# Four graph-attention layers on one core: folding by TensorE, and an order written out for ScalarE and TensorE in the list stage

## The chip, the core and the metric

The kernel runs on one core of a Trainium2 chip. The core has five engines that run side by side and meet at semaphores: TensorE (PE; its weight loads are shown as PEld), VectorE (DVE), ScalarE (ACT), GpSimd (POOL) and SyncE (SP), which here only issues DMAs. Each engine works through its own instructions in order. ScalarE's queue issues DMAs too. The metric is the time of one execution on the device in microseconds; smaller is better. The profile shows one execution, and line numbers such as L698 are those of the kernel before.

## The reference

There are N = 3327 nodes with 512 features and a symmetric adjacency matrix with about 17 entries a row, with ones on the diagonal. Four attention layers follow each other. Each computes

```
h = relu(layernorm(x))
v = h @ W                                  # per head
e[i, j] = leaky_relu(s_src[i] + s_dst[j])  # s_src = v . a_src, s_dst = v . a_dst, per head
x = x + softmax over the neighbours j of i (e) @ v     # layers 1 and 2 pass it through elu
```

with 8, 4, 1 and 8 heads. Since `s_src` is linear in `h`, it can be had as `h @ (W a_src)`: a product of the weights with the attention vectors, done once, gives eight more weight columns for each of the two vectors. The kernel calls this folding.

## The kernel before

Rows are padded to 3328 = 26 tiles of 128. The kernel has a list stage and then, if no row has too many neighbours, four layers that gather neighbours' rows by lists. Only the list stage and the folding of layer 0 are touched by the change.

**The list stage** runs once over the 26 tiles. For tile t SyncE loads 128 rows of the adjacency matrix (`a`, 1664 KB, three buffers; L697). GpSimd multiplies it by descending numbers (`key`, three buffers; L698), so that a row's largest keys name its neighbours. VectorE adds a boost to the diagonal block (L702) and takes the eight largest of each of 16 segments (L707). The 40 largest of those candidates (`top`, L662 and L664) are found in the next tile's loop: the pieces of `rest` stand between the sixteen maxima of the tile after. ScalarE counts the row's ones (L704, with an accumulator) and copies the list (L632, L633). VectorE marks the row's length in one of 41 bins (L640), TensorE counts rows by length with four small products (L642 to L646; the profile shows each product of fp32 as two records), ScalarE copies the running count `sofar` (L649), and VectorE picks each row's place (L654) one tile later still. A buffer of `a` is free again when L698 and L704 have read it.

**Beside the lists**, the same loop computes layer 0's projection. ScalarE's queue loads the tile's x (L726) into one of five row buffers `vx`, ScalarE takes mean and variance (L488 to L495), TensorE transposes (L454), ScalarE cuts at zero (`hT`, L461), TensorE multiplies by the weights (L472), GpSimd raises the variance to the power -1/2 (`root`, L434), ScalarE scales the product by it (L683, L685) and SyncE stores the row to the table `tabx` (L687), from which layer 0 gathers later. In iteration t this is written for tile t-1, behind the maxima of tile t. The weights come in iteration 1 and are folded right there by VectorE: eight times a multiply (L408) and a sum (L410) before tile 2.

**What sets the order.** Inside `with tc.manual_schedule(engines=...)` the engines named keep the order of the source. In the list stage these are GpSimd and VectorE. The order of the others (TensorE, ScalarE, SyncE) is chosen at compile time by a planner that estimates when each instruction is ready. In iteration t GpSimd's order is product t, then the root of t-1. After the loop VectorE finishes the last tile's list and the running count becomes the base of each bin (L738), then ranks, then the lists by rank (L781 to L791). The first gather of layer 0 (L838) needs those.

Of the kernel before, what the change touches and what calls it, by code (L numbers as in the profile page):

```python
# [25 lines left out]
BANK = 512  # L26
# [354 lines left out]
class Weights:  # L381

    def __init__(self, nc, pool, work, l, ws, avs):
# [5 lines left out]
        self.av = pool.tile([P, 2, F], F32, name="av", bufs=1)  # L391
        for s in range(2):
            nc.sync.dma_start(self.w[:, :, s, :HF],
                              ws[l][:, s * HF:(s + 1) * HF].rearrange("(k p) n -> p k n", p=P))
            nc.sync.dma_start(self.av[:, s, :], bass.AP(tensor=avs[l].tensor, offset=avs[l].offset + s * F,
                                                        ap=[[0, P], [1, F]]))
        if self.H < 8:
            nc.vector.memset(self.w[:, :, :, HF + self.H:], 0.0)
        self.left = [(s, k) for s in range(2) for k in range(KC)]

    def fold(self):

# [27 lines left out]
def rooted(nc, ve, small, half=None):  # L430

    if half is not None:
        rstd = small.tile([P, 1], F32, name="root")
        nc.gpsimd.tensor_tensor(rstd, ve, half, OP.pow)  # L434
# [12 lines left out]


def turned(nc, xn, ident, ps_t):

    KC = xn.shape[1] // P
    pt = ps_t.tile([P, KC, P], F32, name="pt")
    for k in range(KC):
        nc.tensor.transpose(pt[:, k, :], xn[:, k * P:(k + 1) * P], ident)  # L454
    return pt


def cut(nc, pt, work):
# [66 lines left out]


@with_exitstack
def tile_gat_stack(ctx: ExitStack, tc: tile.TileContext, x, adj, adjT, ws, avs, out):

# [9 lines left out]
    nc = tc.nc  # L539
    NP, F = x.shape  # L540
    N = adjT.shape[0]
    NT = NP // P
# [21 lines left out]
    with ExitStack() as c1:  # L564
# [19 lines left out]
        nc.scalar.activation(boost, ident, AF.Copy, scale=BOOST)  # L584
# [53 lines left out]
        def sorted_in(t):  # L638
            nonlocal sofar, count
            nc.vector.tensor_scalar(o[:, t, :], bins, held[:, t:t + 1], None, OP.is_equal)  # L640
            pn = ps_n.tile([P, BANK], F32, name="pn", bufs=1)
            nc.tensor.matmul(pn[:, :BINS], upper, o[:, t, :], start=True, stop=False)  # L642
            nc.tensor.matmul(pn[:, :BINS], ident, sofar, start=False, stop=True)
            count = ps_n.tile([P, BANK], F32, name="count", bufs=1)[:, :BINS]
            nc.tensor.matmul(count, ones, o[:, t, :], start=True, stop=False)
            nc.tensor.matmul(count, ident, sofar, start=False, stop=True)  # L646
            if t < NT - 1:
                sofar = once.tile([P, BINS], F32, name="sofar", bufs=2)
                nc.scalar.activation(sofar, count, AF.Copy)  # L649
            return pn  # L650

        def placed(t, pn):
# [27 lines left out]
        def features(t, vx, xn, ve):  # L680
            pv = projected(nc, W, cut(nc, turned(nc, xn, ident, ps_t), work), ps_v)
            rstd = rooted(nc, ve, small, half)
            nc.scalar.activation(vx[:, :ROW].rearrange("p (s n) -> p s n", s=2), pv[:, :, :ROW // 2], AF.Copy,  # L683
                                 scale=rstd)
            nc.scalar.activation(vx[:, ROW + F:].rearrange("p (s n) -> p s n", s=2), pv[:, :, ROW // 2 - 8:ROW // 2],  # L685
                                 AF.Copy, scale=rstd)
            nc.sync.dma_start(tabx[t * P:(t + 1) * P, :], vx)  # L687

        rows = [once.tile([P, 2 * ROW], F32, name=f"vx{i}") for i in range(5)]
        count, pieces, last, normed = None, [], None, None  # L690
        with tc.manual_schedule(engines={mybir.EngineType.Pool, mybir.EngineType.DVE}):
            for t in range(NT):
                a = apool.tile([P, NP], I32, name="a")
                key = kpool.tile([P, NP], I32, name="key")
                quarter = NP // 4 if t == 0 else NP
                for c in range(0, NP, quarter):
                    nc.sync.dma_start(a[:, c:c + quarter], adj[t * P:(t + 1) * P, c:c + quarter])  # L697
                    nc.gpsimd.tensor_tensor(key[:, c:c + quarter], a[:, c:c + quarter], keys[:, c:c + quarter], OP.mult)  # L698
                if t == 1:
                    W = Weights(nc, wpool, work, 0, ws, avs)  # L700
                dg = key[:, t * P:(t + 1) * P]
                nc.vector.tensor_add(dg, dg, boost)  # L702
                waste = once.tile([P, NP], mybir.dt.bfloat16, name="waste")
                nc.scalar.activation(waste, a, AF.Relu, accum_out=total[:, t:t + 1])  # L704
                cand = small.tile([P, SEGS * 8], F32, name="cand")
                for g in range(SEGS):
                    nc.vector.max(cand[:, g * 8:(g + 1) * 8], key[:, g * SEG:(g + 1) * SEG])  # L707
                    if g == SEGS // 2 and last is not None:
                        last()
                        last = None  # L710
                    elif g > 0 and pieces:
                        pieces.pop(0)()
                if t == 0:
                    constants()
                if t == 1:
                    while W.left:
                        W.fold()
                if t == 2:
                    own = late_constants()
                if t > 0:  # L720
                    last = then
                pieces, then = rest(t, cand)

                vx = rows[t % 5]
                xt = vx[:, ROW:ROW + F]
                nc.scalar.dma_start(xt, x[t * P:(t + 1) * P, :])  # L726
                if normed is not None:
                    features(*normed)
                normed = (t, vx, *centred_by_scalar(nc, xt, small, work))
            features(*normed)  # L730
# [754 lines left out]
```

## Time and profile before

| what | value |
|---|---|
| time, median of 3 runs | 2424.75 us (2415.73 to 2427.66) |
| time of the profiled execution | 2419.54 us |
| its span | 2417.8 us |
| PE busy | 2068.3 us (86%) |
| DVE busy | 1885.1 us (78%) |
| POOL busy | 1739.5 us (72%) |
| ACT busy | 936.3 us (39%) |
| first product L698 of the list stage starts | 5.20 us |
| last product L698 starts, takes | 233.80 us, 7.28 us |
| base of the bins (L738) | 253.44 us |
| first gather (L838) | 271.24 us |

In the profile a line gives an engine, the line of the kernel, the operation with what it writes and reads, and a count; "idle before" is the time in which the engine stood still just before, with the instruction that let it go. "issue" is time in which the engine waited for nothing that the profile shows. Busy shares are means over stages with different limits, so the list stage is read by itself.

### The profile page before, as it was taken

How to read it: one execution, taken by the hardware profiler on the slowest of the kernel's cores; microseconds unless marked ns; L12 is line 12 of the kernel's file. 1: busy time of each engine (PE TensorE's matmuls, PEld its weight loads, DVE VectorE, ACT ScalarE, POOL GpSimd, SP SyncE). 2: the span in 40 equal slices, each digit the busy share in tenths (PEclk: the TensorE clock that was granted, in tenths of full speed). 3: DMA queues.
4: the chain of work that ended last, by engine and by line, in shares of the span. 5: the costliest groups of instructions: out<-in, count | busy, mean ns of one | idle time of the engine just before them, and what ended most of it. 6: DMA issues, size and time to landing. Idle time of an engine off the chain costs nothing.

```text
span 2417.8 us, 27489 instructions
## 1 busy us (share of the span) xinstructions
PE 2068.3 (86%) x7298; PEld 1197.0 (50%) x7298; DVE 1885.1 (78%) x4857; ACT 936.3 (39%) x2528; POOL 1739.5 (72%) x1717
## 2 busy tenths in 40 slices
PE   2778779888988885898999987899898699999997
PEld 1656334444444432454455544456565465556653
DVE  7988788877777763888888884888878578888886
ACT  5777113434331111433333332544443444344430
POOL 7899267777777776766677772778778467777775
PEclk9988899999999997999999998999999899999999
DMA  5887569999998788887888884889887578888885
GB/s 227 316 299 248 153 192 299 276 299 282 286 283 237 234 231 241 242 245 235 234 261 255 256 237 141 270 262 283 268 248 240 161 226 256 250 243 246 252 241 176
DMA packets 260732, 594.23 MB, mean 246 GB/s; under 512 B 103699, under 2 KB 121107, under 8 KB 256214
## 3 DMA queue, kind: packets, MB, share of 16 engines
q0 software_dynamic: 124368, 432.13, 59.5%
q1 hardware_dynamic: 132454, 153.45, 19.6%
q10 hardware_dynamic: 3744, 6.82, 0.8%
q8 instruction: 59, 0.97, 0.2%
q14 instruction: 107, 0.88, 0.1%
HBM read 542.60 MB, written 49.65 MB: 245 GB/s over the span
## 4 chain that ended last, share of the span: by engine, by line
DVE 31%; DMA 17%; PE 16%; issue 13%; POOL 12%; ACT 9%; DVEq 0%; SPq 0%; ACTq 0%; POOLq 0%
DVE m L931 13%; POOL g L838 8%; DMA g<-tab,idxb 6%; PE bank L936 5%; DMA g<-tabx,twiceb 4%; PE pv L472 4%; PE whole L1173 3%; POOL key L698 3%; DVE bank L924 3%; ACT r L1280 2%; DMA g<-tab,idxa 2%; DVE room L1296 2%; DVE z L902 2%; ACT pw L903 2%; DVE z L900 1%
## 5 line engine op out<-in xcount | busy, mean ns | idle before, releaser
L936 PE MATMUL bank<-m,ident 128*128 128x512 f32 x2414 | 1128.0, 613 | 144.8 <-DVE m L931 144.3
L838 POOL DMA_INDIRECT g<-tab,idxb x712 | 683.1, 959 | 236.0 <-issue 162.0
L931 DVE TENSOR_TENSOR m<-g,pw 128x512 f32<-128x512 f32 x1207 | 752.2, 682 | 100.2 <-ACT pw L903 99.6
L936 PEld LDWEIGHTS bank<-m,ident 128*128 128x128 f32 x2414 | 448.7, 194 | 689.2 <-issue 314.6
L472 PE MATMUL pv<-w,hT 128*128 128x264 f32 x1664 | 431.5, 413 | 67.8 <-ACT hT L461 44.5
L903 ACT ACTIVATE pw<-z 128x32 f32<-128x32 f32 (+4 forms) x356 | 68.2, 191 | 988.9 <-DVE z L902 988.9
L472 PEld LDWEIGHTS pv<-w,hT 128*128 128x128 f32 x1664 | 331.7, 203 | 166.8 <-ACT hT L461 50.8
L838 POOL DMA_INDIRECT g<-tab,idxa x297 | 286.3, 964 | 165.0 <-issue 110.6
L838 POOL DMA_INDIRECT g<-tabx,twiceb x342 | 324.0, 947 | 106.0 <-issue 79.5
L1173 PE MATMUL whole<-ve,em 128*128 128x512 f32 x468 | 217.8, 612 | 16.3 <-DVE em L1152 11.2
L698 POOL TENSOR_TENSOR key<-a,keys 128x3328 int32<-128x3328 int32 (+1 forms) x29 | 189.3, 6530 | 16.3 <-DVE cand L707 11.8
L924 DVE SCALAR_TENSOR_TENSOR bank<-g,L,bank 128x512 f32<-128x512 f32 x243 | 183.3, 754 | 6.8
L900 DVE TENSOR_TENSOR z<-g,pw 128x32 f32<-128x32 f32 (+4 forms) x356 | 62.6, 176 | 152.1 <-DMA g<-tabx,twiceb 64.7
L1314 PEld LDWEIGHTS whole<-L,room 128*128 128x128 f32 x1248 | 147.5, 190 | 24.9 <-issue 19.1
L838 POOL DMA_INDIRECT g<-tabx,twicea x99 | 94.9, 959 | 78.5 <-issue 38.1
L1314 PE MATMUL whole<-L,room 128*128 128x130 f32 x1248 | 147.8, 274 | 0.0
L707 DVE MAX8 cand<-key 128x8 f32<-128x208 int32 x416 | 144.0, 364 | 0.1
L1173 PEld LDWEIGHTS whole<-ve,em 128*128 128x128 f32 x468 | 88.1, 196 | 109.2 <-issue 87.2
L1280 ACT ACTIVATE r<-low,L 128x384 f32<-128x384 f32 x208 | 121.2, 583 | 5.1
L454 PE MATMUL pt<-ident,xn 128*128 128x128 f32 x416 | 65.4, 281 | 35.4 <-ACT hT L461 13.6
L454 PEld LDWEIGHTS pt<-ident,xn 128*128 128x128 f32 x416 | 52.5, 145 | 68.6 <-issue 28.3
L931 DVE TENSOR_TENSOR bank<-g,pw 128x512 f32<-128x512 f32 x74 | 51.5, 696 | 37.4 <-ACT pw L903 36.6
(180 smaller groups left out, 2192.6 us busy)
## 6 DMA issues: line engine op xcount, KB each, us to landing
a<-in_adj SPq DMA_DIRECT2D x25, 1664.0 KB
tab<-v SPq DMA_DIRECT2D x78, 264.0 KB
ve<-tab SPq DMA_DIRECT2D x78, 264.0 KB
g<-tab SPq DMA_DIRECT2D x65, 264.0 KB
tabx<-vx SPq DMA_DIRECT2D x26, 528.0 KB
g<-tab,idxb POOLq DMA_INDIRECT x712, 4.0
low<-tab SPq DMA_DIRECT2D x52, 132.0 KB
spare<-tab SPq DMA_DIRECT2D x52, 132.0 KB
```

The costliest lines, as they stand in the source:

```text
L454: nc.tensor.transpose(pt[:, k, :], xn[:, k * P:(k + 1) * P], ident)
L472: nc.tensor.matmul(pv[:, s, :HF + 8], hT[:, k, :], W.w[:, k, s, :], start=(k == 0), stop=(k == KC - 1))
L698: nc.gpsimd.tensor_tensor(key[:, c:c + quarter], a[:, c:c + quarter], keys[:, c:c + quarter], OP.mult)
L707: nc.vector.max(cand[:, g * 8:(g + 1) * 8], key[:, g * SEG:(g + 1) * SEG])
L838: nc.gpsimd.indirect_dma_start(out=out_, out_offset=None, in_=table, in_offset=bass.IndirectOffsetOnAxis(ap=which, axis=0))
L903: nc.scalar.activation(self.wt[:, k0:k0 + n, :H], z, AF.Exp)
L924: nc.vector.scalar_tensor_tensor(acc, v, w, acc, OP.mult, OP.add)
L931: nc.vector.tensor_tensor(out_.rearrange("p (s h d) -> p s h d", s=2, d=D), v.rearrange("p s (h d) -> p s h d", d=D), wt[:, k0 + q, :H].re ...
L936: nc.tensor.matmul(self.po, ident, m[:, q, :], start=False, stop=(k0 + q == K - 1), skip_group_check=True)
L1173: nc.tensor.matmul(tl.po.rearrange("p (s m) -> p s m", s=2), e[:, q * P:(q + 1) * P], v.rearrange("p (s m) -> p s m", s=2)[:, :, :F // 2], ...
L1280: nc.scalar.activation(self.r[:, h, :], self.a[:, g, :], AF.Relu, bias=-1.0, scale=self.b[:, j, g:g + 1])
L1314: nc.tensor.matmul(dst, e[:, h, q * P:(q + 1) * P], mov, start=False, stop=(j == NT - 1), skip_group_check=True)
```

## The change

There are three parts.

1. *Folding.* `Weights` gets an argument `turned`. With it no attention vectors are spread over all partitions by DMA; instead the weights are loaded a second time in the other orientation (`wT`, into the buffer `low`, which is not used yet), with a small block-diagonal matrix of the attention vectors (`spread`, made from the inputs like the other rearrangements). `multiply` forms the folded columns by 16 products on TensorE and four copies on ScalarE. It is used for layer 0; the other layers fold as before.
2. *Order.* The whole list stage keeps the source's order on ScalarE and TensorE too, which were the planner's. The source is rearranged for that: the boost first, x of tile t+1 issued in iteration t, projection of t-1 ahead of tile t's maxima, tile t's row total and centring behind it. SyncE stays with the planner.
3. *Later store.* The root, the scaling and the store of a row move from tile t-1 to tile t-2, and so does the copy of the running count, out of `sorted_in` into `passed`. Roots follow product t on GpSimd.

```diff
@@ class Weights
+        if turned is not None:
+            room, wT, spread = turned
+            self.wT = room[:, :KC * F].rearrange("p (c f) -> p c f", c=KC)
+            self.spread = room[:, KC * F:KC * F + KC * 4].rearrange("p (c a) -> p c a", c=KC)
+            nc.sync.dma_start(self.spread, spread.rearrange("p (c a) -> p c a", c=KC))
+            nc.sync.dma_start(self.wT, wT.rearrange("(c p) f -> p c f", p=P))
...
+    def multiply(self, bank):
...
+        for k in range(KC):
+            for c in range(KC):
+                nc.tensor.matmul(pf[:, k, :, c * per:(c + 1) * per], self.wT[:, c, k * P:(k + 1) * P],
+                                 self.spread[:, c, :2 * per].rearrange("p (s h) -> p s h", s=2), start=True, stop=True)
+        for k in range(KC):
+            nc.scalar.activation(self.w[:, k, :, HF:HF + H], pf[:, k], AF.Copy)
@@ list stage
+        def given(t):
+            if t < NT:
+                nc.scalar.dma_start(rows[t % 5][:, ROW:ROW + F], x[t * P:(t + 1) * P, :])
...
+        def passed(t):
+            nonlocal sofar
+            if t < NT - 1:
+                sofar = once.tile([P, BINS], F32, name="sofar", bufs=2)
+                nc.scalar.activation(sofar, counts.pop(t), AF.Copy)
...
-        with tc.manual_schedule(engines={mybir.EngineType.Pool, mybir.EngineType.DVE}):
-            for t in range(NT):
+        with tc.manual_schedule(engines={mybir.EngineType.Pool, mybir.EngineType.PE,
+                                         mybir.EngineType.DVE, mybir.EngineType.Activation}):
+            nc.scalar.activation(boost, ident, AF.Copy, scale=BOOST)
+            given(0)
+            for t in range(NT + 1):
+                if t < NT:
...
+                        nc.sync.dma_start(a[:, c:c + quarter], adj[t * P:(t + 1) * P, c:c + quarter])
+                        nc.gpsimd.tensor_tensor(key[:, c:c + quarter], a[:, c:c + quarter], keys[:, c:c + quarter], OP.mult)
+                    given(t + 1)
+                if t >= 2:
+                    rooted_row(t - 2)
+                    stored(t - 2)
+                    passed(t - 2)
                 if t == 1:
-                    W = Weights(nc, wpool, work, 0, ws, avs)
+                    W = Weights(nc, wpool, work, 0, ws, avs, (low.rearrange("p a b -> p (a b)"), *sums))
+                if t >= 1:
+                    hT = cut(nc, turned(nc, centred_[t - 1][0], ident, ps_t), work)
                 if t == 1:
-                    while W.left:
-                        W.fold()
+                    W.multiply(ps_i.tile([P, BANK], F32, name="pi"))
+                if t >= 1:
+                    pv_[t - 1] = projected(nc, W, hT, ps_v)
+                if t < NT:
+                    waste = once.tile([P, NP], mybir.dt.bfloat16, name="waste")
+                    nc.scalar.activation(waste, a, AF.Relu, accum_out=total[:, t:t + 1])
+                    centred_[t] = centred_by_scalar(nc, rows[t % 5][:, ROW:ROW + F], small, work)
+                    if t == 0:
+                        constants()
...
+            rooted_row(NT - 1)
+            stored(NT - 1)
```

`rooted_row(t)` is the root of L434, `stored(t)` the two scalings and the store of L683 to L687. The diagonal's boost, the sixteen maxima and the pieces follow in the same iteration as before.

More of the change, by code (lines that the diff above doesn't have):

```diff
@@ L381, with __init__ @@
 class Weights:
-    def __init__(self, nc, pool, work, l, ws, avs):
+    def __init__(self, nc, pool, work, l, ws, avs, turned=None):
         F = ws[l].shape[0]
@@ L390, in __init__ @@
         self.w = pool.tile([P, KC, 2, HF + 8], F32, name="w")
-        self.av = pool.tile([P, 2, F], F32, name="av", bufs=1)
+        if turned is None:
+            self.av = pool.tile([P, 2, F], F32, name="av", bufs=1)
         for s in range(2):
@@ L394, in __init__ @@
                               ws[l][:, s * HF:(s + 1) * HF].rearrange("(k p) n -> p k n", p=P))
-            nc.sync.dma_start(self.av[:, s, :], bass.AP(tensor=avs[l].tensor, offset=avs[l].offset + s * F,
-                                                        ap=[[0, P], [1, F]]))
+            if turned is None:
+                nc.sync.dma_start(self.av[:, s, :], bass.AP(tensor=avs[l].tensor, offset=avs[l].offset + s * F,
+                                                            ap=[[0, P], [1, F]]))
+        if turned is not None:
[4 more added lines that the diff above has]
+            nc.sync.dma_start(self.wT, wT.rearrange("(c p) f -> p c f", p=P))
         if self.H < 8:
             nc.vector.memset(self.w[:, :, :, HF + self.H:], 0.0)
-        self.left = [(s, k) for s in range(2) for k in range(KC)]
+        self.left = [(s, k) for s in range(2) for k in range(KC)] if turned is None else []
+    def multiply(self, bank):
+        nc, HF, H = self.nc, self.HF, self.H
+        KC = self.wT.shape[1]
+        per = H // KC
+        pf = bank[:, :KC * 2 * H].rearrange("p (k s h) -> p k s h", k=KC, s=2)
+        for k in range(KC):
[4 more added lines that the diff above has]
+            nc.scalar.activation(self.w[:, k, :, HF:HF + H], pf[:, k], AF.Copy)
     def fold(self):
@@ L527, in tile_gat_stack @@
 @with_exitstack
-def tile_gat_stack(ctx: ExitStack, tc: tile.TileContext, x, adj, adjT, ws, avs, out):
+def tile_gat_stack(ctx: ExitStack, tc: tile.TileContext, x, adj, adjT, ws, avs, sums, out):
     nc = tc.nc
@@ L583, in tile_gat_stack @@
         ahead, boost, bins, one = fixed[:, :P], fixed[:, P:2 * P], fixed[:, 2 * P:2 * P + BINS], fixed[:, 298:299]
-        nc.scalar.activation(boost, ident, AF.Copy, scale=BOOST)
         ones = once.tile([P, P], F32, name="ones")
@@ L643, in sorted_in @@
             nc.tensor.matmul(pn[:, :BINS], ident, sofar, start=False, stop=True)
-            count = ps_n.tile([P, BANK], F32, name="count", bufs=1)[:, :BINS]
+            count = counts[t] = ps_n.tile([P, BANK], F32, name="count", bufs=1)[:, :BINS]
             nc.tensor.matmul(count, ones, o[:, t, :], start=True, stop=False)
             nc.tensor.matmul(count, ident, sofar, start=False, stop=True)
-            if t < NT - 1:
-                sofar = once.tile([P, BINS], F32, name="sofar", bufs=2)
-                nc.scalar.activation(sofar, count, AF.Copy)
             return pn
@@ L678, in check, with rooted_row, stored @@
             nc.vector.tensor_reduce(wrong[:, 1:2], m1, AX.X, OP.add)
-        def features(t, vx, xn, ve):
-            pv = projected(nc, W, cut(nc, turned(nc, xn, ident, ps_t), work), ps_v)
-            rstd = rooted(nc, ve, small, half)
+        rows = [once.tile([P, 2 * ROW], F32, name=f"vx{i}") for i in range(5)]
+        centred_, pv_, root_ = {}, {}, {}
+        def given(t):
+            if t < NT:
+                nc.scalar.dma_start(rows[t % 5][:, ROW:ROW + F], x[t * P:(t + 1) * P, :])
+        def rooted_row(t):
+            root_[t] = rooted(nc, centred_[t][1], small, half)
+        def stored(t):
+            vx, pv, rstd = rows[t % 5], pv_.pop(t), root_.pop(t)
             nc.scalar.activation(vx[:, :ROW].rearrange("p (s n) -> p s n", s=2), pv[:, :, :ROW // 2], AF.Copy,
@@ L687, in features @@
             nc.sync.dma_start(tabx[t * P:(t + 1) * P, :], vx)
-        rows = [once.tile([P, 2 * ROW], F32, name=f"vx{i}") for i in range(5)]
-        count, pieces, last, normed = None, [], None, None
-        with tc.manual_schedule(engines={mybir.EngineType.Pool, mybir.EngineType.DVE}):
-            for t in range(NT):
[L693 to L698, printed above, removed]
-                if t == 1:
-                    W = Weights(nc, wpool, work, 0, ws, avs)
[L701 to L714, printed above, removed]
-                if t == 1:
-                    while W.left:
-                        W.fold()
[L718 to L730, printed above, removed]
@@ new lines, in passed @@
+        def passed(t):
[3 more added lines that the diff above has]
+                nc.scalar.activation(sofar, counts.pop(t), AF.Copy)
+        count, pieces, last, then, counts = None, [], None, None, {}
+        with tc.manual_schedule(engines={mybir.EngineType.Pool, mybir.EngineType.PE,
[4 more added lines that the diff above has]
+                if t < NT:
+                    a = apool.tile([P, NP], I32, name="a")
+                    key = kpool.tile([P, NP], I32, name="key")
+                    quarter = NP // 4 if t == 0 else NP
+                    for c in range(0, NP, quarter):
+                        nc.sync.dma_start(a[:, c:c + quarter], adj[t * P:(t + 1) * P, c:c + quarter])
[5 more added lines that the diff above has]
+                    passed(t - 2)
+                if t == 1:
+                    W = Weights(nc, wpool, work, 0, ws, avs, (low.rearrange("p a b -> p (a b)"), *sums))
+                if t >= 1:
+                    hT = cut(nc, turned(nc, centred_[t - 1][0], ident, ps_t), work)
+                if t == 1:
+                    W.multiply(ps_i.tile([P, BANK], F32, name="pi"))
[7 more added lines that the diff above has]
+                        constants()
+                    dg = key[:, t * P:(t + 1) * P]
+                    nc.vector.tensor_add(dg, dg, boost)
+                    cand = small.tile([P, SEGS * 8], F32, name="cand")
+                    for g in range(SEGS):
+                        nc.vector.max(cand[:, g * 8:(g + 1) * 8], key[:, g * SEG:(g + 1) * SEG])
+                        if g == SEGS // 2 and last is not None:
+                            last()
+                            last = None
+                        elif g > 0 and pieces:
+                            pieces.pop(0)()
+                    if t == 2:
+                        own = late_constants()
+                    if t > 0:
+                        last = then
+                    pieces, then = rest(t, cand)
@@ L1452, in pair, with spread @@
         return np.ascontiguousarray(np.stack([np.asarray(a).reshape(-1), np.asarray(b).reshape(-1)]))
+    def spread(*pair):
+        out = np.zeros((F // P, P // D0, D0, 2, P // D0), np.float32)
+        for s, a in enumerate(pair):
+            for i in range(P // D0):
+                out[:, i, :, s, i] = np.asarray(a).reshape(F // P, P // D0, D0)[:, i]
+        return np.ascontiguousarray(out.reshape(F // P, P, -1).transpose(1, 0, 2)).reshape(P, -1)
     W0, W3 = np.asarray(L0_gnn_W), np.asarray(L3_gnn_W)
     a2, a3 = np.asarray(L2_gnn_attn), np.asarray(L3_gnn_a)
-    F, d3 = W0.shape[1], W3.shape[2]
+    F, d3, D0 = W0.shape[1], W3.shape[2], np.asarray(L0_gnn_a_src).shape[1]
     N = np.asarray(x).shape[0]
@@ L1468 @@
         "w3": np.ascontiguousarray(W3.transpose(1, 0, 2)).reshape(F, -1),
+        "w0t": W0,
+        "s0": spread(L0_gnn_a_src, L0_gnn_a_dst),
         "a0": pair(L0_gnn_a_src, L0_gnn_a_dst),
@@ L1481 @@
         tile_gat_stack(tc, aps["in_x"], aps["in_adj"], aps["in_adjT"], [aps[f"in_w{l}"] for l in range(4)],
-                       [aps[f"in_a{l}"] for l in range(4)], out)
+                       [aps[f"in_a{l}"] for l in range(4)], [aps["in_w0t"], aps["in_s0"]], out)
     r = run_bass_kernel_spmd(nc, [arrays], core_ids=[0])
```

## The prediction

> **What bounds the kernel now.** I read the busy time by stretches first, to see how far the list stage reaches: it is the part that loads adjacency rows, and it fills the first tenth of the span. The columns are the stretch, its length, busy us (instructions) of PE, PEld, DVE, ACT and POOL, the granted clock, the DMA share and GB/s.
>
> ```profile
> 40.00:60.00 20.00, 8.26 (x15) 4.12 (x16) 19.69 (x33) 2.31 (x5) 11.07 (x4) 1.00 0.06 24
> 80.00:100.00 20.00, 13.30 (x69) 11.01 (x67) 18.86 (x95) 17.14 (x33) 19.67 (x5) 0.91 0.92 337
> 180.00:200.00 20.00, 15.41 (x64) 12.33 (x62) 18.23 (x89) 15.37 (x34) 16.66 (x6) 0.80 0.98 333
> ```
>
> Two things are to be seen. From 40 to 60 us DMA is all but idle (24 GB/s) while DVE is "busy" throughout; later POOL, DVE and DMA are all near full. The timeline says what the early hole is:
>
> ```profile
> 35.67 6.88 DVE L408 TENSOR_TENSOR prod<-w,av 128x512 f32<-128x512 f32 x1
> 43.31 7.36 DVE L408 TENSOR_TENSOR prod<-w,av 128x512 f32<-128x512 f32 x1
> 55.64 0.28 DVE L702 TENSOR_TENSOR key<-key,fixed 128x128 int32<-128x128 int32 x1
> 62.84 7.27 POOL L698 TENSOR_TENSOR key<-a,keys 128x3328 int32<-128x3328 int32 x1 [11.77 <-DVE cand L707]
> ```
>
> The folds hold DVE from 29.41 to 55.64, 26.2 us; two of their multiplies (0.69 us at other times) last as long as POOL's product beside them. So DVE starts tile 2 late, the three key buffers stay full, and POOL's sixth product (tile 5) waits 11.77 us. From there POOL runs 20 periods to its last start at 233.80: (233.80 - 62.84)/20 = 8.55 us a tile. Its own floor is shorter: one product 7.26 and one root 0.55, which overlap a little, so that undisturbed starts lie 7.74 apart (131.30, 139.04). The waits of 60 to 235 us give the difference:
>
> ```profile
> POOL root L434 <- ACT ve L495: 11.4, 6, 4.6
> ACT waste L488 <- DMA vx<-in_x: 10.9, 8, 2.3
> SPq L687 <- ACT vx L685: 104.8, 16, 23.9
> ```
>
> POOL's root for tile t-1 stands ahead of the next product and waits for ScalarE's variance, which waits for x. DVE needs 7.03 us a tile (62.68, 69.71, 76.73), less than POOL. After the last product (233.80 + 7.28 = 241.08) the count of the last tile leads to the ranks and the gathers:
>
> ```profile
> 252.09 0.42 PE L642 MATMUL pn<-o,upper 128*128 128x41 f32 x2 [2.95 <-DVE o L640]
> 253.44 0.24 DVE L738 TENSOR_TENSOR_SCAN base<-ones,count 128x41 f32<-128x41 f32 x1 [0.77 <-PE count L646]
> ```
>
> Everything later (2164 us) keeps its work and should move as one piece with the scan at L738.
>
> **The change: the folds.** Eight multiplies and eight sums leave DVE, 26.2 us of its time. They don't all come off the end: POOL's floor takes over as soon as the hole is closed. TensorE gets 16 products, which the trace shows as pairs, so 32 records of a 128x128 weight load and four columns. The nearest rows are the 128x41 ones: eight in 1.90 us at 28.53 (0.24 each, after an idle stretch), eight in 0.98 us at 127.85 (0.122 each). So 3.9 to 7.7 us. The Trainium skill ("TensorE: Matmul & The Clock Gate", Part 1: The HAM clock gate) says that an idle array runs at half clock for about 3.4 us of activity and then at full: 14 records slow and 18 fast, an estimate of 5.6 us. By the slow row it is 7.7. I take 7.7, because transposes six us earlier did not keep it fast here, and POOL hides either: the copies (four of 0.27) then tile 1's row total have to end before tile 4's load is late, not before POOL's next product. The new transposed weights are 1.05 MB instead of 0.52 MB of spread vectors; at 345 GB/s (0 to 20 us) the 0.53 MB cost 1.5 us, if they land ahead of tile 2's row. Two x loads fewer stand ahead of it, 0.5 MB. Between nothing and 3 us, taken: 1.1.
>
> POOL's start then is: product 1 ends at 15.08 + 7.24 = 22.3 as before, product 2 starts at 25.3 (24.25 before), its root 0.55, the late constants 2.55 (31.42 to 33.97), product 3 from 35.6 to 42.9. If the weights arrive so late that ScalarE holds tile 1's row total until 36, tile 4's load is late by 2 us; I charge **1 us** for that.
>
> **The change: root two tiles later.** On POOL the root of t-2 now follows the product of t. Its variance was computed a tile and more before, so the 11.4 us of waits go. Nothing else on POOL waits for ScalarE, and 22 periods from product 3 to product 25 come at 7.74 to 7.9. I take **7.8**: the last product ends at 42.9 + 22 x 7.8 = 214.5, against 241.08. Gain **26.6**.
>
> **The change: ScalarE's fixed order.** After product t ends (call it p), ScalarE's queue is: x of t+1 issued, the row of t-2 scaled behind the root, the running count, the cut of t-1, the row total of a, the centring of t, then the two list copies of t-1. In durations: 0.55 root + 0.74 + 0.10 + 0.50 + 3.06 and hops make 5.3, when the row total lets go of the a buffer; centring 2.3 and copies 0.4 end at p + 8. The next start is at p + 7.74 + 0.55 = 8.3, so ScalarE (7.1 us of work in a period) fits with 0.3 us to spare. Queued behind its wait for the root are the x load of the tile after next and the row totals; POOL waits for them only through a. That is the price: before, a of t+3 was issued when product t ended (146.33, 154.57); now SP waits for ScalarE, 5.3 us longer. It must land when product t+3 can start, at p + 2 x 7.74 + 0.6 = 16.1, so in **10.8 us**. How long does it take?
>
> ```profile
> 85.20 0.47 SPq L697 DMA_DIRECT2D a<-in_adj  x1
> 95.28 7.28 POOL L698 TENSOR_TENSOR key<-a,keys 128x3328 int32<-128x3328 int32 x1
> 131.62 0.33 ACTq L726 DMA_DIRECT2D vx<-in_x  x1
> 140.56 0.63 ACT L488 ACTIVATE waste<-vx 128x512 f32<-128x512 f32 x1 [2.19 <-DMA vx<-in_x]
> ```
>
> Tile 9's row was issued at 85.20 and used at 95.28 without a wait for it, so it took at most 10.1 us with DMA 0.92 busy; tile 10's (93.8, 103.25) at most 9.45. The skill ("DMA: Bandwidth & Descriptors", Anatomy of one DMA) puts a load at 2.0 us plus bytes over 436 GB/s: an estimate of 5.9 us for 1.70 MB and 2.6 for x. The x row above took 8.9. By the rule the margin is 4.9 us, by the row 1.35; I take the row. With 9.45 the loop product, root, ScalarE, load gives (7.26 + 5.3 + 9.45)/3 = 7.3 us a tile, still under 7.74. Bytes: 1.704 + 0.541 + 0.262 = 2.507 MB a tile, 7.4 us at 337 GB/s. POOL stays the bound, with little air: hence 7.8, not 7.74. The boost copy now stands ahead of all x loads on ScalarE: x of tile 0, issued at 0.80 and landed at 5.25 before, goes out near 5 and lands near 9.5, and is used behind the row total that ends at 13.3, so that is hidden. x now has 12.8 us (issued at p + 0.2, used at p + 13) for its 8.9; without that cover ScalarE would stop about 2 us a tile, as the longest waits above.
>
> **The change: SP's queue.** The row of t-2 is stored behind ScalarE's scaling at p + 1.9, a of t+3 behind the row total at p + 5.3. Each is waited for in ScalarE's own order, so that the store stands ahead of the load and costs it nothing. The five row buffers still suffice: x of t+1 waits for the store of t-4, issued two periods earlier.
>
> **The change: TensorE's fixed order.** Per tile: four transposes 0.60, projection 3.83 (218.08) to 5.51 (224.61), eight counting records 0.98 to 1.7. A loop runs cut, projection, counting, transposes, cut: 0.6 + 3.83 + 0.98 + 0.60 + 0.2 = 6.2, with everything slow 8.6. Mean PE time from 80 to 240 us is 6.4 a tile, with the cut 7.1: covered by 7.74.
>
> At the end this order costs. Projection 25 now stands ahead of the last count. ScalarE reaches cut 25 at p + 9.4, it ends at 9.9; projection to 13.8 or 15.5, counting 1.7: 15.5 to 17.2 against 12.4 now (253.44 - 241.08). Loss **3.3**. The last store follows, but the gathers that need it start 17 us after the scan.
>
> **Sum.** 26.6 - 3.3 - 1.0 = 22.3 us. The profiled execution took 2419.54 us (span 2417.8), which gives 2397.2; its time lies 5 us under the median of 2424.75. I forecast **2398**.
>
> **The rivals.** *The pace doesn't improve:* loads of a land after 11 to 12.5 us, or TensorE goes slow after each short idle (8.6 a tile). The 0.98 DMA share at 180 to 200 speaks for it, the 9.45 against. With 8.3 to 8.6 a tile the last product ends at 225.5 to 232, gain 5 to 11, so 2408 to 2415.
>
> *SP's order turns against it, slower:* SP's queue isn't in the source's hands, and if the store of t-1 stands ahead of the load of t+3, that load is issued after product t+1, root, scaling and issue, 2 us, and only one product can run meanwhile: two periods are 9.3 + d, with d the time to land. At 9.45 that is 9.4 a tile: 42.9 + 206 = 249, and 2431. It decides from 8.8 a tile (d = 8.3), where gain and tail cancel. For it: stores pile up in the queue now (the 104.8 us above). Against: the readiness follows ScalarE's order.
>
> *The change does more:* 7.74 exact, no startup charge, tail 2: last product 213.2, gain 26, 2393; if the weights come early too, 2388.
>
> **How the numbers follow.** Chances: forecast 0.68 (2389 to 2406), unchanged pace 0.17, SP's order 0.10, more 0.05. A measurement here can tell about 0.5%, 12 us, so faster means under 2412.6. The forecast nearly whole, half of the second and the last give faster 0.77; same 0.13; slower 0.10. Range 2386 to 2415: what is left out is the slower case and the ends.
>
> **What would show it.** Right: no L408 ahead of 55 us; DVE tile 2 begins near 33; POOL starts 7.7 to 7.9 apart, waits for ve near zero; last product ends near 214; the scan 15 to 17 us behind it. Wrong: POOL waiting for a from in_adj tile after tile, or loads of a standing behind the next store.

## The result, and the profile after

The changed kernel takes 2392.13 us (median of 4 runs, 2389.89 to 2394.43); the kernel before took 2425.71 us beside it (4 runs, 2415.73 to 2427.66). The ratio is 0.987, 95% interval 0.9841 to 0.9899. In a second comparison (`after_again`, below) it is 0.9873 (0.9853 to 0.9892). The forecast was 2398 us, range 2386 to 2415.

The two profiled executions took 2419.54 and 2394.43 us (spans 2417.8 and 2392.7), a difference of 25.1 us where the sum of the prediction has 22.3. The medians differ by 33.6 us (30.9 in the second comparison), because the unprofiled runs of the kernel before lie 5 to 8 us above its profiled one, except for one at 2415.73. None of the long ones was profiled, so that difference stays unexplained.

The busy time by stretches of the changed kernel, with the same columns as before (stretch, length, PE, PEld, DVE, ACT, POOL, granted clock, DMA share, GB/s):

```profile
40.00:60.00 20.00, 13.92 (x61) 11.25 (x60) 17.27 (x85) 17.01 (x39) 20.00 (x7) 0.82 0.82 308
80.00:100.00 20.00, 14.85 (x65) 11.77 (x64) 18.56 (x91) 17.98 (x34) 20.00 (x7) 0.85 0.92 342
180.00:200.00 20.00, 14.91 (x81) 12.03 (x80) 18.16 (x89) 18.61 (x38) 20.00 (x7) 0.99 0.95 342
```

The hole at 40 to 60 us is gone: DMA moves 308 GB/s there where it moved 24. POOL is busy for 20.00 of 20 us in all three stretches. ScalarE comes to 18.6 of 20 us in the last one, where it had 15.4.

The timeline of the changed kernel (start, us, what ran; in brackets the idle time before it and what ended it), in three excerpts: the start, one tile in the middle, the end.

```profile
19.46 6.96 PE L417 MATMUL pi<-low 128*128 128x4 f32 x32 [3.67 <-DMA low<-in_w0t]
23.90 7.24 POOL L733 TENSOR_TENSOR key<-a,keys 128x3328 int32<-128x3328 int32 x1 [3.46 <-DMA a<-in_adj]
26.46 0.41 ACT L420 ACTIVATE w<-pi 128x16 f32<-128x16 f32 x4 [8.98 <-PE pi L417]
26.70 6.64 PE L493 MATMUL pv<-w,hT 128*128 128x264 f32 x16 [0.27 <-ACT w L420]
34.21 7.25 POOL L733 TENSOR_TENSOR key<-a,keys 128x3328 int32<-128x3328 int32 x1
41.94 7.27 POOL L733 TENSOR_TENSOR key<-a,keys 128x3328 int32<-128x3328 int32 x1
...
128.05 0.32 SPq L713 DMA_DIRECT2D tabx<-vx  x1
131.62 0.33 SPq L732 DMA_DIRECT2D a<-in_adj  x1
142.49 7.36 POOL L733 TENSOR_TENSOR key<-a,keys 128x3328 int32<-128x3328 int32 x1
...
204.33 7.42 POOL L733 TENSOR_TENSOR key<-a,keys 128x3328 int32<-128x3328 int32 x1
221.03 3.83 PE L493 MATMUL pv<-w,hT 128*128 128x264 f32 x16 [0.69 <-ACT hT L482]
225.71 0.24 DVE L777 TENSOR_TENSOR_SCAN base<-ones,count 128x41 f32<-128x41 f32 x1 [0.24 <-PE count L666]
```

At the start, the folding is 32 records on TensorE in 6.96 us, and ScalarE stands still 8.98 us for the transposed weights and for it. POOL waits once for a whole row of adjacency (3.46 us) and from product 3 (34.21) goes straight on. In the middle, SP issues the store first and the load of the row 3.6 us after it; the row is used at 142.49, 10.87 us after its issue, with no wait. At the end, projection 25 (221.03) stands between the last product and the base of the bins (225.71). Three lines of the waits of the changed kernel from 50 to 205 us (us in all, times, longest):

```profile
PE pv L493 <- ACT hT L482: 29.8, 20, 2.3
DVE key L754 <- POOL key L733: 12.2, 20, 0.6
ACT vx L709 <- POOL root L455: 8.3, 16, 0.6
```

POOL has no line in that view. The other engines wait for it, each tile anew, by half a microsecond: POOL is the bound, and the 11.4 us in which its root waited for the variance are gone.

By places in the list stage, all from the timelines ("product 5" is the sixth row; pace is the distance of products 5 to 25, divided by 20; e1, e2 and e9 are experiments told below):

| | product 5 | product 25 | pace | base of bins |
|---|---|---|---|---|
| before | 62.84 | 233.80 | 8.55 | 253.44 |
| e1: fold on TensorE, order of before | 60.79 | 232.56 | 8.59 | 251.96 |
| e2: order of after, fold on VectorE | 65.89 | 222.42 | 7.83 | 243.82 |
| e9: e1 with ScalarE storing | 50.82 | 267.24 | 10.82 | 287.84 |
| after | 49.66 | 204.33 | 7.73 | 225.71 |

So of the 29.5 us that the last product starts earlier, 13.2 are the hole and 16.3 the pace. From there to the base of the bins it is 21.38 us against 19.64, a loss of 1.7. From the base to the first gather it is 18.62 against 17.80, and from the gather to the end 2148.4 against 2146.6, losses of 0.8 and 1.8: 29.5 - 1.7 - 0.8 - 1.8 = 25.2, which is the difference of the spans but for rounding.

### The profile page after: what moved, and what is told of

Its sections match the earlier page's. It is cut to its first block, busy times and chain, and to the rows that moved or that the text cites. A ratio compares the mean times of both kernels' runs of the same rounds, so it can differ in the third digit from the quotient of the medians.

```text
span 2392.7 us, 27548 instructions
## 1 busy us (share of the span) xinstructions
PE 2072.6 (87%) x7330; PEld 1203.9 (50%) x7330; DVE 1859.2 (78%) x4841; ACT 944.5 (39%) x2532; POOL 1736.7 (73%) x1717
## 4 chain that ended last, share of the span: by engine, by line
DVE 27%; DMA 18%; POOL 17%; issue 15%; PE 14%; ACT 8%; DVEq 0%; SPq 0%; POOLq 0%; ACTq 0%
DVE m L970 12%; POOL g L877 10%; DMA g<-tab,idxb 7%; PE bank L975 5%; POOL key L733 5%; DMA g<-tabx,twiceb 5%; PE whole L1212 3%; DMA g<-tab,idxa 3%; PE pv L493 3%; DVE bank L963 2%; ACT r L1319 2%; DVE z L941 1%; ACT pw L942 1%; DVE room L1335 1%; PE pi L828 1%
## 5 line engine op out<-in xcount | busy, mean ns | idle before, releaser
L493 PE MATMUL pv<-w,hT 128*128 128x264 f32 x1664 | 422.5, 411 | 46.6 <-ACT hT L482 42.9
L877 POOL DMA_INDIRECT g<-tabx,twiceb x342 | 323.7, 946 | 106.5 <-issue 80.7
L1212 PE MATMUL whole<-ve,em 128*128 128x512 f32 x468 | 220.2, 618 | 15.4 <-DVE em L1191 10.2
```

The source lines that it names most:

```text
L877: nc.gpsimd.indirect_dma_start(out=out_, out_offset=None, in_=table, in_offset=bass.IndirectOffsetOnAxis(ap=which, axis=0))
L1212: nc.tensor.matmul(tl.po.rearrange("p (s m) -> p s m", s=2), e[:, q * P:(q + 1) * P], v.rearrange("p (s m) -> p s m", s=2)[:, :, :F // 2], ...
```

## The experiments

**The kernel before once more (e0).** No edit; it shows how well a profile repeats.

> The kernel before, unchanged, in another execution. If the list stage of before is what varies from one execution to the next (its waits for ScalarE and DMA depend on chance), the scan of the bins comes several us away from 253.4 us. If the later layers vary, it comes within 1 us of 253.4 and the span differs from 2417.8 behind it.

Measured: 2420.01 us, last product 233.25, base of the bins 253.11, first gather 271.37. All four agree with the first profile within 0.6 us, so differences of one or two microseconds at these places can be read. Single products in between differ by up to 2.1 us.

**The fold alone (e1).** The kernel before with the folding of the changed one. TensorE, ScalarE and SP keep the planner's order.

```diff
-                    W = Weights(nc, wpool, work, 0, ws, avs)
+                    W = Weights(nc, wpool, work, 0, ws, avs, (low.rearrange("p a b -> p (a b)"), *sums))
...
-                    while W.left:
-                        W.fold()
+                    W.multiply(ps_i.tile([P, BANK], F32, name="pi"))
```

> The kernel before with TensorE's folding alone; order and store as before. Theory (two causes): the early hole closes, product 3 ends near 42, but the products stay about 8.4 to 8.6 us apart because POOL's root still stands behind ScalarE's variance, so the last one ends at 227 to 232 us: some 10 us less than before, and 18 more than the changed kernel. Rival (the fold is all of it): products 7.75 us apart, last one ends near 213, as fast as the changed kernel.

Measured: ratio 0.9979 (0.9966 to 0.9992), 2417.07 us against 2420.99. The gain is some 4 us; the folds themselves had held VectorE for 26. The hole is still there, with another cause. The timeline of e1:

```profile
34.47 2.97 ACT L725 ACTIVATE waste<-a 128x3328 bf16<-128x3328 int32 x1
...
44.96 6.08 SPq L708 DMA_DIRECT2D tabx<-vx  x2
51.13 0.38 SPq L718 DMA_DIRECT2D a<-in_adj  x1
...
60.79 7.22 POOL L719 TENSOR_TENSOR key<-a,keys 128x3328 int32<-128x3328 int32 x1 [10.02 <-DMA a<-in_adj]
```

The row total at 34.47 is the third, tile 2's, and the last reader of the buffer that tile 5's row goes into: free at 37.5. The load is issued at 51.13, directly behind two stores of projected rows, and product 5 waits 10.02 us for it. In the changed kernel the same load goes out at 38.23. The planner had put those stores ahead of the load in SP's queue, so that the load waits for a projection that it has nothing to do with.

Also the pace stays at 8.59, though POOL's root waits for a variance only once, by 0.8 us, after 69 us: POOL's products wait 6.6 us for rows instead, and another 9.3 us are put down to VectorE. One of these, at tile 7:

```profile
69.44 0.32 SPq L708 DMA_DIRECT2D tabx<-vx  x1
69.86 0.38 SPq L718 DMA_DIRECT2D a<-in_adj  x1
...
79.16 7.24 POOL L719 TENSOR_TENSOR key<-a,keys 128x3328 int32<-128x3328 int32 x1 [2.90 <-DVE cand L728]
```

VectorE was done with this product's key buffer at 57.4, so it isn't what POOL waited for. The row's buffer was free at 50.3, but its load went out at 69.86, directly behind a store, and the row was used 9.3 us later. It is the same with the other such waits: the rows of tiles 5 to 15 and of tile 17 were issued 9.7 to 19.6 us after their buffer was free, each directly behind a store. From product 5 to product 17 the pace is 9.08 us; from there on, where the rows are issued 11.6 us or more ahead of their use, it is 7.85. So late rows took the place of late variances: one wait was taken away and another came up behind it.

**The order alone (e2).** The changed kernel, folding on VectorE as before.

```diff
-                    W = Weights(nc, wpool, work, 0, ws, avs, (low.rearrange("p a b -> p (a b)"), *sums))
+                    W = Weights(nc, wpool, work, 0, ws, avs)
...
-                    W.multiply(ps_i.tile([P, BANK], F32, name="pi"))
+                    while W.left:
+                        W.fold()
```

> The changed kernel with VectorE's folding back. Theory (two causes): the hole stays, some 13 to 20 us of it reach the end, but behind it the products come 7.73 us apart; the last one ends at 218 to 232 us, and no root waits for a variance: 12 to 18 us less than before. Rival (the fold is all of it): last product at 236 or later, less than 5 us gained.

Measured: ratio 0.9942 (0.9926 to 0.9959), 2407.75 us. The timeline of e2:

```profile
22.92 7.13 DVE L429 TENSOR_TENSOR prod<-w,av 128x512 f32<-128x512 f32 x1
...
52.95 7.26 POOL L733 TENSOR_TENSOR key<-a,keys 128x3328 int32<-128x3328 int32 x1 [11.76 <-DVE cand L758]
```

The hole is the old one, with two of VectorE's eight multiplies as long as the product beside them and POOL waiting 11.76 us for a free key buffer; product 5 then waits 4.62 us more for its row. Behind it the pace is 7.83. So the order gives the pace without the fold, as expected, and the hole needs the fold *and* an order of SP in which loads don't queue behind early stores. The parts alone give some 4 and 13 us, together 31 (2423.33 to 2392.45 in the second comparison). They don't add up, because the hole has two causes and goes only when both are gone: product 5 starts 2 us earlier with the fold alone, 3 us later with the order alone, and 13.2 us earlier with both.

**SP's stores out of the way (e9).** To test e1's cause, one edit on top of e1: the store goes from SP's queue into ScalarE's.

```diff
-            nc.sync.dma_start(tabx[t * P:(t + 1) * P, :], vx)
+            nc.scalar.dma_start(tabx[t * P:(t + 1) * P, :], vx)
```

> TensorE's folding alone (the planner's order on ScalarE and TensorE, store one tile later), with one more edit: the row's store is issued by ScalarE's queue instead of SyncE's. Theory (folding alone gained little because in SyncE's queue each row's store, which waits for ScalarE, stood ahead of the load of a): the loads go out when a buffer is free, products come 7.75 to 8.2 us apart, the last one ends at 215 to 222 us, time 2396 to 2405, over 12 us less than folding alone. Rival (ScalarE's order by the planner is the brake in itself, by late variances and row totals): 8.5 us a tile or more, time above 2412.

Measured: ratio 1.0159 (1.0142 to 1.0176), 2458.39 us: slower, so the expectation was wrong. But the part that was asked for is seen: products 3 to 6 start at 35.37, 43.08, 50.82 and 58.55, 7.73 apart. Without stores ahead of the loads the hole is closed. Then the pace becomes 10.8 us. The waits of e9 from 60 to 265 us:

```profile
POOL root L455 <- ACT ve L516: 42.9, 10, 8.4
ACT kept L653 <- DVE top L683: 42.5, 10, 6.4
```

The edit gave ScalarE one more kind of instruction, the planner ordered ScalarE anew, and now copies that wait for a list stand ahead of the variance that POOL waits for. So e9 supports e1's cause of the hole. What the pace of e1 would be with SP's order alone repaired it can't say, because ScalarE's order changed as well; what held it up to product 17 is seen in e1's own timeline.

**The store one tile later instead of two (e3).** Root, scaling and store of t-1 straight behind its projection.

```diff
-                    rooted_row(t - 2)
-                    stored(t - 2)
...
+                    rooted_row(t - 1)
+                    stored(t - 1)
...
```

> The changed kernel with root, scaling and store one tile after the tile instead of two, straight behind its projection. Theory (the second tile is what lets ScalarE run on): ScalarE waits for the projection, 4 to 5.5 us, ahead of its row total, so a period becomes cut 0.5, projection 4 to 5, scaling 0.75, row total 3.1, centring 2.3, copies 0.4: 11 to 12 us a tile, the scan comes near 300 us and the time is 65 to 95 us above the changed kernel. Rival (only the written order matters): 7.73 us a tile as in the changed kernel.

Measured: 2540.41 us in a single run, beside 2420.99; products 13.65 us apart. The direction was as expected, the size larger. The timeline of e3:

```profile
143.25 0.70 ACT L709 ACTIVATE vx<-pv,root 128x528 f32<-128x528 f32 x1 [6.25 <-PE pv L493]
149.22 0.20 ACT L516 ACTIVATE ve<-squares 128x1 f32<-128x1 f32 x1
149.50 0.55 POOL L455 TENSOR_TENSOR root<-ve,half 128x1 f32<-128x1 f32 x1 [5.92 <-DVE junk L655]
150.02 7.22 POOL L733 TENSOR_TENSOR key<-a,keys 128x3328 int32<-128x3328 int32 x1
```

ScalarE waits 6.25 us for a projection that has just begun. The variance queued behind it ends at 149.4, and POOL's root, which takes it, starts right then (the instruction named in brackets is not what the root reads). Then the next product starts and with it the next projection: everything runs one after the other.

**One tile later, but nothing waited for that has just begun (e3b).** Root of t-1 behind product t, scaling and store behind the centring of t.

```diff
-                    rooted_row(t - 2)
-                    stored(t - 2)
...
+                if t >= 1:
+                    rooted_row(t - 1)
...
+                    if t >= 1:
+                        stored(t - 1)
...
```

> As the changed kernel, but root, scaling and store one tile after the tile, with the scaling behind the centring of the next tile in ScalarE's order. Theory (what counts is that nothing is waited for that was only just begun, not two tiles as such): the projection has ended by then, the root follows its variance by about 0.4 us, so products stay 7.73 to 7.9 us apart and the time is within 5 us of the changed kernel. Rival (two tiles are needed): POOL's root waits for the variance again, 8.2 us a tile or more, over 10 us slower than the changed kernel.

This and the next three ran on another chip, on which the kernel before takes 2925.19 us. The changed kernel did not run there, so whole times can't be set beside its own, and the same 30 us are a smaller share. The times of the list stage are comparable, since its products are as far apart as on the other chips. Measured: ratio to the kernel before 0.9919 (0.9884 to 0.9954); products 7.73 apart, the last at 205.56, base of the bins at 226.22. So the second tile of distance isn't what pays. The place in ScalarE's queue is: the scaling stands where its projection is done in most tiles. In 20 tiles of e3b ScalarE waits for a projection 5 times, 2.6 us in all; in 17 tiles of e3 each time, 106.5 us in all.

**SP's order turned against it (e4).** The rival of the prediction, made on purpose: SP in the source's order, with the store of t-2 followed by the load of t+2. That puts the store of t-1 ahead of the load of t+3.

```diff
+        with tc.manual_schedule(engines={mybir.EngineType.Pool, mybir.EngineType.PE, mybir.EngineType.SP,
...
+            load(0)
+            load(1)
...
                     stored(t - 2)
+                load(t + 2)
```

> The changed kernel with SyncE's order written out too, so that the store of tile t-1 stands ahead of the load of tile t+3 (three buffers as before; weights behind tile 3's load). My rival of the prediction: two periods are 9.3 us plus the landing time d of a row of a, so with d at most 9.45 up to 9.4 us a tile, the last product up to 249 us, time up to 2431. If a load lands as fast as the rule of the Trainium skill for its bytes says (5.9 us), two periods are 15.2, under POOL's own floor, and nothing changes but the start.

Measured: 2933.79 us beside 2925.19, base of the bins at 254.49. Product 4 starts only at 52.34, since in this order the weights land late; from 60.06 to 233.46 the pace is 8.67. The timeline of e4:

```profile
112.26 0.32 SPq L713 DMA_DIRECT2D tabx<-vx  x1
112.67 0.38 SPq L733 DMA_DIRECT2D a<-in_adj  x1
121.11 7.27 POOL L743 TENSOR_TENSOR key<-a,keys 128x3328 int32<-128x3328 int32 x1 [1.08 <-DMA a<-in_adj]
```

The mechanism is the one that the rival named, and its price is 8.67 - 7.73 = 0.94 us a tile. From 60.5 us on POOL waits 17.9 us: 6.9 are put down to rows, the rest to VectorE, which had itself just waited for POOL and has nothing to do with the row's buffer. It also measures what could only be bounded: the row shown was used 8.44 us after its issue and waited for; the 20 rows issued from 61 us on have 7.5 to 9.2, and the rival's own formula (two periods are 9.3 + d) gives 8.0. In the changed kernel the row has 10.87, so there are some 1.7 to 3.4 us to spare. The whole time is within 0.3% of the kernel before, in a single run.

**The count ahead of the last projection (e5).**

```diff
-                if t >= 1:
+                if 1 <= t < NT:
                     hT = cut(nc, turned(nc, centred_[t - 1][0], ident, ps_t), work)
...
+            pv_[NT - 1] = projected(nc, W, hT, ps_v)
```

> The changed kernel with the last tile's projection behind the last count on TensorE. Theory (the projection stands ahead of the count at the end): the scan comes 11.5 to 12.7 us behind the last product's end instead of 14.2, 1.5 to 2.5 us less time if the last store doesn't hold the ranks. Rival (the store sets it): ranks are written only when the last store has landed, and the first gather comes no earlier.

Measured: ratio 0.9883 (0.9846 to 0.992). From the last product to the base of the bins it is 20.19 us against 21.38 and 21.06 in the changed kernel, so 0.9 to 1.2 us less. But the first gather stands 39.64 us behind the last product, against 40.0 and 38.17. The timeline of e5 says why nothing arrives:

```profile
221.10 7.89 SPq L713 DMA_DIRECT2D tabx<-vx  x2
224.08 0.24 DVE L778 TENSOR_TENSOR_SCAN base<-ones,count 128x41 f32<-128x41 f32 x1 [1.18 <-PE count L666]
231.38 0.37 SPq L784 DMA_DIRECT2D tabx<-rank  x1
```

The ranks are found at 227.98. Their write follows the last store in SP's queue and waits until that has landed (2.2 us in SP's waits), and the last store now waits for a projection that comes later: it goes out at 228.67 instead of 225.84. So the write goes out at 231.38, where in the changed kernel it is 228.79. No gain of the whole is shown.

**The late constants out of the loop (e7).** POOL's fill of some constants moves behind the 26 tiles.

```diff
-                    if t == 2:
-                        own = late_constants()
...
+            own = late_constants()
```

> The changed kernel with the 2.6 us of late constants on POOL moved from tile 2 to the end of the loop. Theory (POOL is the bound of the whole list stage): every later product starts 2.6 us earlier and the time falls by 2 to 2.6 us. Rival (DMA is as tight): the products then wait for rows of a, and the last one ends less than 1 us earlier.

Measured: ratio 0.9886 (0.9842 to 0.9929). Product 3 starts at 31.25 instead of 34.21 and the last at 201.46, 2.7 to 2.9 us earlier than in the changed kernel. The base of the bins is at 222.48, against 225.71 and 225.23. What is taken from POOL at the start arrives whole at the end of the list stage: POOL is the bound there. Whether the whole time falls by as much isn't shown.

**The changed kernel again (after_again), and two roots at once (e6).** One power of 128x2 every second tile instead of two of 128x1.

```diff
+            if t % 2 == 0:
+                both = small.tile([P, 2], F32, name="root")
+                nc.gpsimd.tensor_tensor(both, ves[t // 2 % 2], half.to_broadcast([P, 2]), OP.pow)
+                root_[t], root_[t + 1] = both[:, 0:1], both[:, 1:2]
...
```

> The changed kernel, unchanged, beside the two versions of this call: 2390 to 2395 us, products 7.73 us apart.

> The changed kernel with one root for two tiles (every second tile). Theory (POOL is the bound): a period falls from 7.73 to about 7.47 us, the last product ends 22 x 0.26 = 5.7 us earlier, time 4 to 6 us less. Rival (DMA, at 0.92 busy and 330 GB/s, or ScalarE with 0.3 us to spare, takes over at once): products wait for a, less than 2 us gained.

Measured: the changed kernel 2392.45 us, ratio 0.9873 (0.9853 to 0.9892), products 7.74 apart, base of the bins at 225.23, first gather 242.34. With roots in pairs 2394.07, ratio 0.9877 (0.9857 to 0.9897), so no gain. The timeline of e6:

```profile
82.16 0.69 POOL L709 TENSOR_TENSOR root<-ve,half 128x2 f32<-128x2 f32 x1 [0.96 <-DVE cand L763]
...
97.24 0.92 POOL L709 TENSOR_TENSOR root<-ve,half 128x2 f32<-128x2 f32 x1
```

The pair costs 0.69 us where two single ones cost 1.1. Yet from 82.81 on the products come 15.1 to 15.5 us apart in pairs, 7.54 to 7.75 a tile where 7.47 was expected; two pairs before that took 15.8 and 16.3 us, and product 3 is late by some 1.5 us, since the first pair needs a second variance. Nine of the thirteen roots show 0.91 to 1.16 us without a named wait; what lengthens them isn't settled.

**All three together (e8)**, the edits of e5, e6 and e7:

```diff
-                if t >= 1:
+                if 1 <= t < NT:
...
+                both = small.tile([P, 2], F32, name="root")
...
+            own = late_constants()
```

> Roots in pairs, late constants at the end and the last count ahead of the last projection, together. If POOL stays the bound the three add up: 8 to 10 us less than the changed kernel. If DMA takes over, the sum stays under 5 us and products wait for rows of a.

Measured: 2389.40 us, ratio 0.9859 (0.9839 to 0.988), last product 201.54, base of the bins 222.24, first gather 241.21. That is the lowest time measured, 3 us under the changed kernel beside it, but the intervals overlap: it isn't shown to be better than the changed kernel.

## Why the prediction was right, and where its numbers were off

**The hole closes.** Right: no folds on VectorE, and products 3, 4 and 5 follow each other without a gap. The step was credited to the fold alone ("POOL's floor takes over as soon as the hole is closed"). There it was incomplete: in e1 a hole of 10.0 us remains, because SP's queue under the planner makes one of its own. The prediction sees stores ahead of loads only as a danger to the pace, not as a second cause of the hole. That the order written out for ScalarE removes it as well was luck; without it the forecast for this step would have failed.

**The folding on TensorE.** The trace has 6.96 us for 32 records. The row taken gave 7.7; the estimate by the half-clock rule of the Trainium skill ("TensorE: Matmul & The Clock Gate", Part 1: The HAM clock gate) gave 5.6, with 14 records at half clock and 18 at full. The trace has no such change of rate: 10 or 11 records fall into each 2 us, 0.2175 us a record, and the projection right behind takes 6.64 us where projection 25 (221.03) takes 3.83. The granted clock in these rows is 1.00 throughout, so a half clock isn't seen in it, and neither is a change after 3.4 us; what keeps TensorE slow here isn't settled. Taking the slow row was right. The folding was hidden, as said: product 3 starts at 34.21 where 35.6 was forecast, because product 2 starts at 23.90 and not at 25.3, so that the 1.1 us for the weights' bytes were not needed, and neither was the charge of 1 us for the start.

**The pace.** 7.73 us against 7.8 forecast, 1.5 us over 22 periods. POOL's floor is the pace, since POOL waits for nothing; e7 shows that POOL's work alone moves the end. The reason given was only half of it. The prediction put the 11.4 us of waiting for the variance down to the root being one tile late. In e1 these waits are nearly gone with the root where it was, and the pace is not better; in e3b the root is one tile late and the pace is 7.73. The pairs e3 and e3b (ScalarE's queue) and the changed kernel and e4 (SP's queue) agree with another reading: POOL keeps its floor where no queue holds a wait for something that has just begun ahead of something that POOL needs next. That the second tile of distance is one way to get there, and not the cause, is shown by e3b.

**ScalarE's queue and the loads.** Right by the numbers: the load goes out 5.1 us after the product ends (131.62 behind 126.5; forecast 5.3), has 10.87 us (forecast 10.8) and is in time. The bound of 9.45 us taken for its landing was a little high: e4 has 7.5 to 9.2. The skill's estimate of 5.9 us ("DMA: Bandwidth & Descriptors", Anatomy of one DMA) was low, by 1.6 to 3.3 us in traffic of 289 GB/s. The formula was carried over to another case: that section fits it to DMAs that GpSimd issues, and these are issued by SP and ScalarE. One landing was put too early: x of tile 0 came at 13.09, not near 9.5, and ScalarE waited 1.61 us for it, at no cost to POOL. So the rival in which the pace doesn't improve had less room than the 0.17 it got.

**SP's queue.** Right: store, then load, each tile, the store 1.5 us after the product (forecast 1.9). The slower rival is real where it is built (e4, 0.94 us a tile), and its formula holds; with 8.0 us to land it stays below the 8.8 us a tile from which it would have decided. One reading behind this rival was wider than said: the 104.8 us of stores waiting for ScalarE, listed with the waits of 60 to 235 us, are those of 0 to 260; from 60 to 235 us they are 63.3 in 12 waits. No sum rests on it.

**The tail.** Right in sign, half in size: 1.7 us lost where 3.3 were charged. Projection 25 ran in 3.83 us, the fast end of what was given, for which the sum has a loss of 3.1. The rest is that the cut ended 9.2 us behind the product and not 9.9, and that the base of the bins followed the projection by 0.85 us where 1.7 was counted.

**What wasn't foreseen.** The way from the base of the bins to the end took 2.6 us more. Its first part, to the first gather, varies from one profile to the next: 17.80 and 18.26 us before, 18.62 and 17.11 after, so no loss is shown there. From the gather to the end it is 2146.6 and 2146.9 before, 2148.4 and 2148.5 after: 1.5 to 1.9 us that repeat. Their cause is left open.

By the terms: the last product 29.5 us earlier (forecast 26.6), the tail -1.7 (-3.3), the start nothing (-1.0), later -2.6 (nothing). That is 25.2 against 22.3. So by its terms the list stage came out as the third rival, *the change does more* (7.74 exact, no charge at the start, tail 2), which had 0.05; the loss behind it, which was not forecast, brought the time back towards the forecast.

## What to carry to other kernels

Two changes can each do next to nothing for a hole alone and close it together: look for what is second in line for the same engine before crediting either. In an in-order queue ask of each instruction whether what it waits for has just begun or is long done; one row scaled too early (e3) made the span 146 us longer than the changed kernel's, and one store ahead of a load (e1) kept a hole of 10 us open. Where one engine is busy without a gap, take work from that engine; a shorter path elsewhere (e5) arrives only if the next queue lets it through.

## What the runs showed of the hardware that was not expected

- A fp32 product of four columns costs nearly as much per record (6.96 / 32 = 0.2175 us) as one of 41 columns did in the slow stretch before (0.24).
- TensorE, busy from 19.46 to 33.3 us but for 0.27 us, ran these records and the projection behind them slowly all the while (6.64 us against 3.83), at a granted clock of 1.00. In e4, where the folding starts at 27.99, the same two take 6.96 and 6.61 us.
- POOL's power takes 0.55 us for 128x1 and, where it starts after a wait, 0.69 us for 128x2 (e6): most of it doesn't grow with the columns.
- A 1.70 MB row was in use 7.5 to 9.2 us after its issue, while a row is stored and x is loaded beside it, at 289 GB/s in all (e4, 20 rows).
- On another chip the same kernel before took 2925.19 us instead of 2420.99, and a list stage with ScalarE's order written out still ran at 7.73 us a tile (e3b): the stage that POOL bounds did not slow down, the rest did. From 500 to 1500 us the granted clock of e3b is 0.84 to 0.85 and its DMA moves 188 to 203 GB/s; the changed kernel in its first profile has 0.94 to 0.97 and 235 to 258. Which of the two slows the rest isn't shown.
